# Layer 1's input convolution on four engines, and its sums of directions inside a list-scheduled output stage

## The chip, the cores and the metric

The kernel runs on one core of one Trainium2 chip. The metric is the device time of one execution in microseconds (us). Before the change three runs took 27333.85, 27416.35 and 27510.57 us, a median of 27416.35 us. One more execution was recorded by the hardware profiler, and every duration below is from that one.

The engines are TensorE (PE, and PEld for its weight loads), VectorE (DVE), ScalarE (ACT), GpSimd (POOL) and SyncE (SP). In this kernel SP issues the DMAs.

## The reference, cut to what matters

Two layers work on an image x of 4 x 128 x 128 pixels with 192 channels. Layer 0 is not touched by the change. Layer 1 is, in all of it but the scan over time:

```python
x = x + layer1(_gn(x))            # _gn: group norm over 32 groups of channels, per batch
# layer1(v):
xz = v @ in_proj_w;  x_ssm, z = xz[..., :C], xz[..., C:]       # C = 192
xc = silu(conv3x3_depthwise(x_ssm) + conv_b)                   # zero padding
# four directions: rows forward, rows backward, columns forward, columns backward
ys = scan(...)                                                 # 16 states a channel
y  = y0 + y1 + y2 + y3            # y2, y3 are scanned by columns, so they are transposed
y  = (y - mean_c(y)) / sqrt(var_c(y) + 1e-5) * ln_g + ln_b     # over the 192 channels
return (y * silu(z)) @ out_w
```

All arithmetic is float32.

## The kernel before, in words

The kernel is a row of stages. `transpose_in` turns the input to channels by pixels. `layer0` does layer 0. Then layer 1 begins: `in_conv` makes the convolved input `xc`, `scans` runs the four directions, `merge` adds the column directions to the row directions, and `layer1_out` does the norm, the gate and the output product. Data goes from stage to stage through DRAM.

Layer 1 has 192 channels, and a tile has 128 partitions. So two batches form a pair (`PAIRS` is 2), and their 2 x 192 channels make three blocks of 128 partitions: block 0 is channels 0 to 127 of the first batch, block 1 is channels 128 to 191 of the first batch in partitions 0 to 63 and those of the second in partitions 64 to 127, and block 2 is channels 0 to 127 of the second batch. A product over channels thus needs several terms for a block, `PAIR_TERMS`: two terms for blocks 0 and 2, three for block 1. The weights of a term are padded with zeros to 128 x 128 (`pair_pack`).

An image of 16384 pixels is cut into 16 chunks (`NCH`) of 8 rows, 1024 pixels (`T`).

`in_conv` loops over 2 pairs, 3 blocks and 16 chunks, so 96 chunks. For each it loads the source blocks with one row above and below, normalises them on VectorE (line 790), makes the product on TensorE (line 805, and line 816 for the two edge rows), copies it into a padded tile `xi` on ScalarE (lines 809 and 820), takes the nine taps of the convolution on VectorE (lines 823 and 829), takes the silu (line 833) and writes the result twice: straight away, and turned into a whole image `img` in memory (line 835), from which the columns are stored (line 839). GpSimd only zeroes the edges of `xi` (line 796).

`merge` loads a whole image of a column direction, and for each chunk loads the row direction, adds the two (line 1228) and stores the sum back. `layer1_out` loops over 2 pairs and 16 chunks, so 32 chunks with all three blocks each. A chunk has a mean over channels (line 210 through `mm`), a subtraction (1264), a square (1265), a mean of the squares (210), Ln and Exp for the inverse root (1270, 1271), a multiplication (1272), scale and shift (1275), the gate z (210, 1282, 1283), and the output product, which also adds x itself through an identity matrix (lines 1291 to 1301).

Work in `in_conv`, `merge` and `layer1_out` is ordered by the program text and by the pools' buffers. `layer0` and `scans` are ordered in another way: each lists its operations with an engine, an assumed cost and the tiles that it reads and writes, and class `Order` plays a list schedule with these costs; `emit` then writes the instructions of each engine in the order found. Each engine runs its own list strictly in order, SP's too: an instruction that waits holds up all behind it.

Of the kernel before, what the change touches and what calls it, by code (L numbers as in the profile page):

```python
# [10 lines left out]
F32 = mybir.dt.float32  # L11
AF = mybir.ActivationFunctionType
# [36 lines left out]
def flat(t):  # L49
    return t.rearrange("p a b -> p (a b)")  # L50


def rows(t):
    return t.rearrange("p (r w) -> p r w", w=W)
# [146 lines left out]
class Maker:  # L201
    def __init__(self, tc):
        self.tc, self.nc = tc, tc.nc

    def mm(self, out, terms):

        nc = self.nc
        for h in range(2):
            for i, (lhsT, rhs) in enumerate(terms):
                nc.tensor.matmul(  # L210
                    out[:, h], lhsT, rhs[:, h * 512 : (h + 1) * 512],
                    start=(i == 0), stop=(i == len(terms) - 1),
                )

    def softplus(self, pool, x, bias):

        l = pool.tile([128, T], F32, tag="sp_l", name="sp_l", bufs=2)
        self.nc.scalar.activation(l, x, AF.Softplus, bias=bias)
        return l
# [544 lines left out]
    def load_gn(self, pool, gn, p):  # L764
        t = pool.tile([128, 3, 2], F32, tag="gn", name="gn")
        for i in range(3):
            self.load_block(t[:, i], gn, p, i, slice(0, 2))
        return t

    def in_conv(self, x1T, gn, xc, win, vec):  # L770

        nc, tc = self.nc, self.tc
        with tc.tile_pool(name="p_1", bufs=1) as p1, tc.tile_pool(
            name="p_2", bufs=2
        ) as p2, tc.tile_pool(name="p_ps", bufs=2, space=PSUM) as ps:
            for p in range(PAIRS):
                gnt = self.load_gn(p2, gn, p)
                for i in range(3):
                    vt = vec[:, i % 2]
                    img = p1.tile([128, W, H], F32, tag="img", name="img")  # L780
                    for j in range(NCH):
                        r0 = R * j
                        lo, hi = max(r0 - 1, 0), min(r0 + R, H - 1)
                        wl, nr = lo - (r0 - 1), hi - lo + 1
                        terms = []
                        for t, src in PAIR_TERMS[i]:
                            xt = p2.tile([128, R + 2, W], F32, tag=f"x{src}", name=f"x{src}")
                            xv = xt[:, wl : wl + nr].rearrange("c r w -> c (r w)")
                            self.load_block(xv, x1T, p, src, slice(lo * W, (hi + 1) * W))
                            nc.vector.tensor_scalar(  # L790
                                xv, xv, gnt[:, src, 0:1], gnt[:, src, 1:2],
                                ALU.subtract, ALU.mult,
                            )
                            terms.append((win[:, t], xt))
                        xi = p2.tile([128, R + 2, W + 2], F32, tag="xi", name="xi")
                        nc.gpsimd.memset(xi[:, :, 0:1], 0.0)  # L796
                        nc.gpsimd.memset(xi[:, :, W + 1 : W + 2], 0.0)
                        if j == 0:
                            nc.gpsimd.memset(xi[:, 0, :], 0.0)
                        if j == NCH - 1:  # L800
                            nc.gpsimd.memset(xi[:, R + 1, :], 0.0)
                        g = ps.tile([128, 2, 512], F32, tag="g", name="g_xi")
                        for h in range(2):
                            for q, (lhsT, xt) in enumerate(terms):
                                nc.tensor.matmul(  # L805
                                    g[:, h], lhsT, xt[:, 1 + 4 * h : 5 + 4 * h],
                                    start=(q == 0), stop=(q == len(terms) - 1),
                                )
                        nc.scalar.copy(
                            xi[:, 1 : R + 1, 1 : W + 1],  # L810
                            g.rearrange("p h (r w) -> p (h r) w", w=W),
                        )
                        g = ps.tile([128, 2, 512], F32, tag="g", name="g_halo")
                        for n, wr in enumerate(wr for wr in (0, R + 1) if wl <= wr < wl + nr):
                            for q, (lhsT, xt) in enumerate(terms):
                                nc.tensor.matmul(
                                    g[:, n, :W], lhsT, xt[:, wr],
                                    start=(q == 0), stop=(q == len(terms) - 1),
                                )
                            nc.scalar.copy(xi[:, wr, 1 : W + 1], g[:, n, :W])  # L820
                        acc = p2.tile([128, T], F32, tag="acc", name="acc")
                        a3 = rows(acc)
                        nc.vector.tensor_scalar(
                            a3, xi[:, 1 : R + 1, 1 : W + 1],
                            vt[:, V1_CW + 4 : V1_CW + 5], None, ALU.mult,
                        )
                        for t in range(9):
                            if t != 4:
                                nc.vector.scalar_tensor_tensor(  # L829
                                    a3, xi[:, t // 3 : t // 3 + R, t % 3 : t % 3 + W],  # L830
                                    vt[:, V1_CW + t : V1_CW + t + 1], a3, ALU.mult, ALU.add,
                                )
                        nc.scalar.activation(acc, acc, AF.Silu, bias=vt[:, V1_CB : V1_CB + 1])
                        nc.sync.dma_start(xc[0][p][i][:, j * T : (j + 1) * T], acc)
                        nc.scalar.copy(
                            img[:, :, r0 : r0 + R], acc.rearrange("p (r w) -> p w r", w=W)
                        )
                    for j in range(NCH):
                        nc.sync.dma_start(
                            xc[1][p][i][:, j * T : (j + 1) * T],  # L840
                            img[:, R * j : R * (j + 1)].rearrange("p w h -> p (w h)"),
                        )
# [367 lines left out]
    def merge(self, y):  # L1210

        nc, tc = self.nc, self.tc
        with tc.tile_pool(name="m_2", bufs=2) as p2, tc.tile_pool(name="m_3", bufs=3) as p3:
            for p in range(PAIRS):
                for i in range(3):
                    img = p2.tile([128, W, H], F32, tag="img", name="img")
                    for c in range(4):
                        w = slice(c * W // 4, (c + 1) * W // 4)
                        nc.sync.dma_start(
                            img[:, w].rearrange("p w h -> p (w h)"),  # L1220
                            y[1][p][i][:, w.start * H : w.stop * H],
                        )
                    for j in range(NCH):
                        cols = slice(j * T, (j + 1) * T)
                        t = p3.tile([128, T], F32, tag="y", name="y")
                        nc.sync.dma_start(t, y[0][p][i][:, cols])
                        t3 = rows(t)
                        nc.vector.tensor_tensor(
                            t3, t3,
                            img[:, :, R * j : R * (j + 1)].rearrange("p w r -> p r w"), ALU.add,  # L1230
                        )
                        nc.sync.dma_start(y[0][p][i][:, cols], t)

    def layer1_out(self, y, x1T, gn, out, wz, avg, wout, vec, ident, eps):
        nc, tc = self.nc, self.tc
        with tc.tile_pool(name="s_2", bufs=2) as p2, tc.tile_pool(
            name="s_ps", bufs=2, space=PSUM
        ) as ps:
            for p in range(PAIRS):
                gnt = self.load_gn(p2, gn, p)  # L1240
                for j in range(NCH):
                    cols = slice(j * T, (j + 1) * T)
                    ys, x1, xn, sqs = [], [], [], []
                    for i in range(3):
                        yt = p2.tile([128, T], F32, tag=f"y{i}", name=f"y{i}")
                        nc.sync.dma_start(yt, y[p][i][:, cols])
                        ys.append(yt)
                        xt = p2.tile([128, T], F32, tag=f"x{i}", name=f"x{i}")
                        self.load_block(xt, x1T, p, i, cols)
                        x1.append(xt)  # L1250
# [248 lines left out]
```

## Time and profile before

| what | value |
|---|---|
| median of three runs | 27416.35 us |
| the profiled execution | 27483.88 us, its span 27482.1 us |
| `in_conv`, first normalisation to last image store | 6138 to 7453 us: 1315 us |
| `scans` | 7453 to 25190 us: 17737 us |
| `merge` | 25190 to 25680 us: 490 us |
| `layer1_out` | 25680 to 27482 us: 1802 us |
| PE busy over the span | 24406.1 us, 89% |
| DVE busy | 22279.5 us, 81% |
| ACT busy | 21227.8 us, 77% |
| POOL busy | 19417.1 us, 71% |

The bounds of the stages are read off the first and last instructions of their lines. The page gives for each group of instructions its line, engine, operation, tiles and shapes, the count, the busy time and the mean of one; matmuls of float32 leave two records each, so a count of 28 records is 14 matmuls. In a list of stretches, each row has the length, then the busy time of each engine with the number of instructions, then the granted TensorE clock as a share of full speed, the share of the DMA engines' time that was used and the rate in GB/s.

### The profile page before, as it was taken

The numbers are of one execution on the slowest core, as the hardware profiler recorded it, in microseconds if no ns is written. First come the engines' busy times: TensorE is split into PE (matmuls) and PEld (weight loads), VectorE is DVE, ScalarE is ACT, GpSimd is POOL, SyncE is SP. The second block draws the span as 40 slices with busy tenths as digits, with TensorE's granted clock in tenths as the row PEclk, the third lists the DMA queues.
The fourth block names the chain that finished last, engine by engine and source line by source line (L and its number), as shares of the span: only waits on it lengthen the run. The fifth ranks groups of instructions, "written<-read, shape, count | busy, mean of one in ns | idle before, by whom it ended". The sixth has DMA issues, their size and how long they took to land.

```text
span 27482.1 us, 440640 instructions
## 1 busy us (share of the span) xinstructions
PE 24406.1 (89%) x169976; PEld 9399.1 (34%) x169976; DVE 22279.5 (81%) x16004; ACT 21227.8 (77%) x24544; POOL 19417.1 (71%) x9258
## 2 busy tenths in 40 slices
PE   5999999994599999999999999999999999996699
PEld 3333333332233333333333333333333333332355
DVE  4888888889888899899888898889998898896222
ACT  5989898963378888788888888888888888884355
POOL 3777777730088888888888898888888888885000
PEclk7999999997789999899999999999999999997899
DMA  7999999995544445444444454444454444455422
GB/s 214 240 237 244 236 244 234 244 219 187 174 122 128 132 133 137 126 127 125 117 126 130 131 138 129 131 131 133 133 138 118 119 121 125 132 135 178 175 83 81
DMA packets 1672336, 4265.04 MB, mean 155 GB/s; under 512 B 239584, under 2 KB 388512, under 8 KB 1667168
## 3 DMA queue, kind: packets, MB, share of 16 engines
q1 hardware_dynamic: 1670240, 4236.84, 57.6%
q8 instruction: 1346, 22.05, 0.4%
q14 instruction: 750, 6.14, 0.1%
HBM read 3296.80 MB, written 939.10 MB: 154 GB/s over the span
## 4 chain that ended last, share of the span: by engine, by line
PE 37%; DVE 19%; ACT 13%; issue 6%; DMA 4%; POOL 2%; SPq 1%; DVEq 0%; POOLq 0%; ACTq 0%
DVE h L1108 13%; PE f L1075 13%; PE Y L1122 10%; ACT h L1086 6%; ACT dA L1102 3%; PE s L929 3%; PE s L952 2%; POOL hc L1114 2%; DVE acc L829 2%; PE hf L590 1%; DMA y<-y 1%; DVE D L1001 1%; PE g_mean L210 1%; DMA C<-cs 1%; PE s L995 1%
## 5 line engine op out<-in xcount | busy, mean ns | idle before, releaser
L1114 POOL TENSOR_TENSOR hc<-h,C 128x1024 f32<-128x1024 f32 x6144 | 14338.8, 2363 | 2382.5 <-PE Y L1122 1149.2
L1108 DVE TENSOR_TENSOR_SCAN h<-dA,st,h 128x1024 f32<-128x1024 f32 x5760 | 13132.8, 2333 | 765.5 <-ACT st L1138 281.2
L1086 ACT COPY h<-f 128x1024 f32<-128x1024 f32 (+3 forms) x8192 | 6334.2, 799 | 2215.8 <-PE f L1075 2144.5
L1075 PE MATMUL f<-D,dT 32*64 32x256 f32 x98304 | 7157.2, 408 | 786.1 <-ACT h L1086 640.4
L1122 PE MATMUL Y<-hc,sel 128*64 128x512 f32 x24576 | 6986.2, 656 | 470.4 <-POOL hc L1114 215.2
L1102 ACT ACTIVATE dA<-d,alog 128x1024 f32<-128x1024 f32 x6144 | 6905.3, 1124 | 312.3 <-DVE h L1108 257.1
L1075 PEld LDWEIGHTS f<-D,dT 32*64 32x64 f32 x98304 | 3276.9, 138 | 6683.6 <-ACT h L1086 4810.8
L468 POOL TENSOR_TENSOR xs<-xs,pr 128x1024 f32<-128x1024 f32 x1536 | 3637.3, 2371 | 341.0 <-ACT pr L463 251.4
L611 DVE SCALAR_TENSOR_TENSOR hf<-hh,vec,hf 128x512 f32<-128x512 f32 x3072 | 2318.3, 755 | 427.3 <-PE hf L590 268.1
L1122 PEld LDWEIGHTS Y<-hc,sel 128*64 128x64 f32 x24576 | 1321.0, 141 | 2966.3 <-issue 1795.9
L590 PE MATMUL hf<-sa,diag 96*32 96x512 f32 x18432 | 2157.4, 601 | 22.6 <-DMA sa<-hpad 20.2
L463 ACT ACTIVATE pr<-xi,vec 128x1024 f32<-128x1024 f32 x1536 | 1714.1, 1143 | 297.2 <-POOL xs L468 291.8
L1001 DVE TENSOR_TENSOR D<-s,mask 128x1024 f32<-128x1024 f32 x1024 | 1240.2, 1211 | 849.7 <-PE s L995 849.7
L590 PEld LDWEIGHTS hf<-sa,diag 96*32 96x32 f32 x18432 | 563.2, 109 | 1490.8 <-issue 1402.1
L796 POOL MEMSET xi<- 128x10 f32 x96 | 24.5, 255 | 1480.5 <-DVE acc L829 1224.5
L805 PE MATMUL g_xi<-x,wx 128*128 128x512 f32 x896 | 545.0, 745 | 590.5 <-DVE x L790 515.6
L550 POOL TENSOR_TENSOR dl<-dl,xs 128x1024 f32<-128x1024 f32 x192 | 454.6, 2368 | 832.8 <-ACT dA L548 745.8
L962 POOL TENSOR_TENSOR u<-l,u 128x1024 f32<-128x1024 f32 x384 | 907.4, 2363 | 184.6 <-ACT l L955 161.7
L829 DVE SCALAR_TENSOR_TENSOR acc<-xi,vec,acc 128x1024 f32<-128x1024 f32 x768 | 959.3, 1280 | 23.2 <-ACT xi L820 9.7
L1108 DVE TENSOR_TENSOR_SCAN h<-dA,h 128x1024 f32<-128x1024 f32 x384 | 856.2, 2274 | 59.5 <-ACT dA L1102 27.6
L952 PE MATMUL s<-pj,w 128*128 128x512 f32 x1536 | 894.2, 665 | 6.9 <-ACT l L955 2.2
L210 PE MATMUL g_mean<-y,avg 128*128 128x512 f32 x896 | 393.5, 596 | 480.3 <-DMA y<-y 480.0
(172 smaller groups left out, 23437.1 us busy)
## 6 DMA issues: line engine op xcount, KB each, us to landing
C<-cs SPq DMA_DIRECT2D x4096, 256.0 KB, 4.8
sa<-hpad SPq DMA_DIRECT2D x2304, 276.0 KB, 7.3
d<-delta SPq DMA_DIRECT2D x1536, 256.0 KB, 4.2
u<-xc SPq DMA_DIRECT2D x384, 512.0 KB, 4.7
delta<-l SPq DMA_DIRECT2D x384, 512.0 KB, 3.8
y<-y SPq DMA_DIRECT2D x1536, 128.0 KB, 3.3
hh<-hpad SPq DMA_DIRECT2D x384, 414.0 KB, 7.8
y<-y SPq DMA_DIRECT2D x288, 512.0 KB, 3.8
```

The source lines that it names most:

```text
L463: op("ACT", 1.1, lambda pr=pr, t=t: nc.scalar.activation(rows(pr()), x()[:, t // 3 : t // 3 + R, t % 3 : t % 3 + W], AF.Copy, scale=v(k, V ...
L468: op("POOL", 2.38, lambda pr=pr: nc.gpsimd.tensor_tensor(o(), o(), pr(), ALU.add), reads=[pr], writes=[o], early=-429)
L590: nc.tensor.matmul(o()[32 * g : 32 * g + 32], diag[:, d, s, k, g], x[:, g, :, c0 : c0 + W], start=(d == 0 and s == 0), stop=(d == 1 and s ...
L611: nc.vector.scalar_tensor_tensor(o3, hh()[:, 1 + dy : 5 + dy, PAD + dx : PAD + dx + W], v(k, V0_K + col), o3, ALU.mult, ALU.add,)
L829: nc.vector.scalar_tensor_tensor(a3, xi[:, t // 3 : t // 3 + R, t % 3 : t % 3 + W], vt[:, V1_CW + t : V1_CW + t + 1], a3, ALU.mult, ALU.add,)
L1001: nc.vector.tensor_tensor(t().rearrange("t a (n s) -> t (a n) s", s=32), g()[:, : 2 * NS].unsqueeze(2).to_broadcast([128, 2 * NS, 32]), ma ...
L1075: nc.tensor.matmul(gs()[64 * jn : 64 * jn + 64, n, 256 * a : 256 * a + 256], td()[rt, r // 64, 2 * sb + a], tD()[rt, a, 256 * jn : 256 * j ...
L1086: nc.scalar.copy(H[:, at : at + nq, 256 * sb : 256 * sb + 256].rearrange("p q (a r s) -> p q a r s", a=2, s=32)[:, :, :, 2 * rp : 2 * rp + 2],
L1102: op("ACT", 1.16, lambda: nc.scalar.activation(a(), d(), AF.Exp, scale=alog[:, c : c + 1]), reads=[d], writes=[a], table="exp", early=-522)
L1108: nc.vector.tensor_tensor_scan(hs[:, way], a()[:, way], hs[:, way], 0.0 if at == 0 else s0()[:, q : q + 1], ALU.mult, ALU.add,)
L1114: op("POOL", 2.4, lambda: nc.gpsimd.tensor_tensor(t(), hs, tC(), ALU.mult), reads=[hq, tC], writes=[t])
L1122: nc.tensor.matmul(ym()[64 * th : 64 * th + 64], sel, t()[:, 512 * th : 512 * th + 512], start=(q == 0), stop=(q == NQ - 1),)
```

## The change

Three stages are replaced by two: `in_conv` is written anew, and `merge` and `layer1_out` become one stage, `outputs`. Both are now ordered by `Order`. `layer0` and `scans` keep their text, and the order of every engine in them is the same as before.

In both stages the group norm is no longer applied to x. `pair_weights` multiplies the weights by the inverse deviation once for each pair, and forms the product of weights and mean, which becomes a bias at the eviction.

In `in_conv` a chunk now loads only eight new rows; the two rows that it shares with its predecessor are copied (`cy`). The nine taps are split: taps 0 and 8 on TensorE with diagonal weights into PSUM, taps 4, 1, 3, 5 and 7 on VectorE, the first of them adding the PSUM result, and taps 2 and 6 as products on ScalarE, which GpSimd adds up and then adds to the sum. The image `img` has two buffers in place of one. The tile `x` has one ring of four buffers for all source blocks.

In `outputs` the mean and the mean of squares are formed for each of the two batches, as 128 equal rows, in place of each of the three blocks: a whole-array matmul for the block of 128 channels, and for block 1 a matmul with the 64 rows of that batch. The two batches' 64-row matmuls follow each other. The gate's projection and the output product use 64-row matmuls for block 1 too, and the projection of block 1 uses two matmuls with 64 columns each. The mean is subtracted straight from PSUM, scale joins the multiplication by the inverse deviation, shift joins the gate. Ln and Exp are grouped for the two batches. `merge` for the first pair comes first, and that for the second pair is placed among the chunks of the first; the image has one buffer.

```diff
+    def pair_project(self, outs, i, terms, xs):
...
+        if i == 1:
+            parts = [(1, slice(0, 128), slice(0, 128)), (0, slice(0, 128), slice(0, 64)),
+                     (2, slice(0, 128), slice(64, 128))]
+        else:
+            parts = [(i, slice(0, 128), slice(0, 128)), (1, slice(32 * i, 32 * i + 64), slice(0, 128))]
+        of = {src: lhsT for lhsT, src in terms[i]}
+        for h, out in enumerate(outs):
+            for q, (src, k, m) in enumerate(parts):
+                nc.tensor.matmul(
+                    out[m], of[src][k, m], xs(src, h)[k], start=(q == 0), stop=(q > 0 if i == 1 else q == 1)
+                )
...
+    def in_conv(self, x1T, gn, xc, win, vec, ident):
...
+        TENSOR, PRODUCTS, VECTOR = (0, 8), (2, 6), (4, 1, 3, 5, 7)
...
+            od = Order(keep=226, idle=0.250, rate=300e3)
...
+                    t = xs[src] = buf("x", 4, 128, R + 1, W)
...
+                op("PE", 3.0, mm, reads=list(xs.values()), writes=[g, t], early=-150)
+                op("POOL", 0.5, edges, writes=[t])
...
+                op("PE", 3.2, taps_mm, reads=[t], writes=[gc])
+                op("DVE", 1.5, lambda: tap(VECTOR[0], flat(gc())), reads=[t, gc], writes=[acc])
+                for q in VECTOR[1:]:
+                    op("DVE", 1.3, lambda q=q: tap(q, acc()), reads=[t], writes=[acc])
+                prs = []
+                for q in PRODUCTS:
+                    pr = buf("pr", 3, 128, T)
+                    op("ACT", 1.12, lambda q=q, pr=pr: nc.scalar.activation(
+                        rows(pr()), shifted(q), AF.Copy, scale=vt[:, V1_CW + q : V1_CW + q + 1]),
+                        reads=[t], writes=[pr], early=30)
+                    prs.append(pr)
+                op("POOL", 2.4, lambda: nc.gpsimd.tensor_tensor(
+                    prs[0](), prs[0](), prs[1](), ALU.add), reads=[prs[1]], writes=[prs[0]])
+                op("POOL", 2.41, lambda: nc.gpsimd.tensor_tensor(
+                    acc(), acc(), prs[0](), ALU.add), reads=[prs[0]], writes=[acc])
+                op("ACT", 1.17, lambda: nc.scalar.activation(
+                    acc(), acc(), AF.Silu, bias=vt[:, V1_CB : V1_CB + 1]), writes=[acc])
+                op("SP", 0.1, lambda: nc.sync.dma_start(
+                    xc[0][p][i][:, j * T : (j + 1) * T], acc()), reads=[acc], size=524e3)
+                op("ACT", 2.02, lambda: nc.scalar.copy(
+                    img()[:, :, R * j : R * j + R], acc().rearrange("p (r w) -> p w r", w=W)
+                ), reads=[acc, img], writes=[(img, j)], early=-237)
...
-    def merge(self, y):
...
-    def layer1_out(self, y, x1T, gn, out, wz, avg, wout, vec, ident, eps):
...
+    def outputs(self, y, x1T, gn, out, win, wo, vec, ident, eps):
...
+            def merge(p, i):
+                img = buf("img", 1, 128, W, H)
...
+                    t = buf("m", 3, 128, T)
...
+                def averages(name, src):
+                    gs = [bank2(name), bank2(name)]
+
+                    def mm():
+                        for h in range(2):
+                            c = slice(512 * h, 512 * h + 512)
+                            for e in range(2):
+                                nc.tensor.matmul(
+                                    gs[e]()[:, h], avg, src[2 * e]()[:, c], start=True, stop=False
+                                )
+                            for e in range(2):
+                                k = slice(64 * e, 64 * e + 64)
+                                nc.tensor.matmul(
+                                    gs[e]()[:, h], avg[k], src[1]()[k, c], start=False, stop=True
+                                )
...
+                                nc.tensor.matmul(
+                                    dst[e], ys[2 * e]()[:, tok], wo[:, 0], start=True, stop=False
+                                )
+                                nc.tensor.matmul(
+                                    dst[e][:, 0:128], x1[2 * e]()[:, tok], ident,
+                                    start=False, stop=False,
+                                )
...
+                                nc.tensor.matmul(
+                                    dst[e], ys[1]()[k, tok], wo[k, 1 + e], start=False, stop=False
+                                )
...
+                                nc.tensor.matmul(
+                                    dst[e][:, 128:C], x1[1]()[k, tok], ident[k, k],
+                                    start=False, stop=True,
+                                )
...
+            for i in range(3):
+                merge(0, i)
+            for p in range(PAIRS):
+                for j in range(NCH):
+                    if p == 0 and j in (1, 6, 11):
+                        merge(1, j // 5)
+                    chunk(p, j)
```

## Prediction

> **What bounds the kernel now.** I first cut the span into stages by the lines of `in_conv`, `scans`, `merge` and `layer1_out`. The stretches give each engine's load.
>
> ```profile
> 6138.00:7453.00 1315.00, 649.27 (x1736) 318.68 (x1736) 1196.35 (x1088) 431.23 (x469) 30.46 (x199) 0.74 0.59 185
> 7453.00:25190.00 17737.00, 16256.19 (x133104) 5996.88 (x133104) 15701.72 (x8193) 14699.00 (x17595) 15210.40 (x6525) 0.94 0.48 128
> 25190.00:25680.00 490.00, 7.63 (x19) 1.46 (x18) 182.44 (x100) 1.12 (x1) 7.84 (x4) 0.50 0.83 313
> 25680.00:27482.00 1802.00, 1746.84 (x6784) 1061.68 (x6783) 424.33 (x384) 993.73 (x928) 0.00 (x0) 1.00 0.28 84
> ```
>
> (Columns: stretch, length, busy PE, PEld, DVE, ACT, POOL, clock, DMA share, GB/s.) Three stages have three bounds: VectorE in `in_conv` (1196 of 1315 us), DMA in `merge` (0.83, compute idle), TensorE in `layer1_out` (1747 of 1802). The change leaves the other 23,875 us as they are, with the same order of instructions, so all is decided in 3607 us: 1315 + 490 + 1802. The groups of the first stage say what VectorE does there:
>
> ```profile
> L829 DVE SCALAR_TENSOR_TENSOR acc<-xi,vec,acc 128x1024 f32<-128x1024 f32 x768 | 959.3, 1280 | 23.2 <-ACT xi L820 9.7 <-DVE acc L829 0.5
> ...
> L835 ACT COPY img<-acc 128x1024 f32<-128x1024 f32 x96 | 191.8, 2004 | 20.5 <-DMA xc<-acc 9.5 <-DMA xc<-img 9.2
> ...
> L790 DVE TENSOR_SCALAR x<-x,gn 128x1280 f32<-128x1280 f32 x196 | 184.3, 941 | 29.1 <-DMA x<-x1T 25.6 <-PE g_halo L816 3.5
> ```
>
> Eight taps a chunk, and 23 us of idle time before all 768: nothing is late. For what a small matmul costs, I read TensorE's timeline in `layer0`, which already runs 32-row matmuls:
>
> ```profile
> 3005.46 1.12 PE L499 MATMUL g<-proj,ident 32*128 32x512 f32 x2
> 3006.51 2.84 PE L649 MATMUL g<-y,avg 128*128 128x512 f32 x6
> ...
> 3017.32 1.13 PE L499 MATMUL f<-proj,ident 32*128 32x512 f32 x4
> 3018.38 2.84 PE L649 MATMUL g<-sq,avg 128*128 128x512 f32 x6
> ```
>
> One such matmul (2 records) takes 1.05 us to the next start, two on different rows (4 records) 1.06: pairs on different rows run together. The mean of `layer1_out`, 14 matmuls in 12.1 us, gives 0.86 us for a whole one. So a change of array shape costs about 0.2 us.
>
> Last, does GpSimd suffer beside VectorE? The edge zeroing of `in_conv` tells:
>
> ```profile
> 6708.38 7.25 DVE L829 SCALAR_TENSOR_TENSOR acc<-xi,vec,acc 128x1024 f32<-128x1024 f32 x6
> 6714.58 0.12 POOL L796 MEMSET xi<- 128x10 f32 x1 [13.76 <-DVE acc L829]
> ...
> 6650.49 0.75 DVE L823 TENSOR_SCALAR acc<-xi,vec 128x1024 f32<-128x1024 f32 x1
> ...
> 6650.72 0.57 POOL L796 MEMSET xi<- 128x10 f32 x1 [9.25 <-DVE acc L829]
> ```
>
> It takes 0.12 us beside a tap with two inputs in memory, and 0.57 beside a multiplication by a constant, until that ends.
>
> **What the Trainium skill says.** "TensorEngine Tiling (Array Packing)", Key Properties: tiles execute in parallel, and changing the mode drains the array. The lines above agree: 1.06 against 1.05, and 0.2 us. "TensorE: Matmul & The Clock Gate", Part 1: TensorE left idle falls to half clock. The stages agree: 0.74 where PE is half idle, 1.00 where full. "ScalarE: Activation LUTs", What ACT_TABLE_LOAD costs: 1283 ns and a drain of 1380; the trace has 1283 ns, and the chain shows no drain behind it. "GPSIMD Engine Reference", Key points: GpSimd contends with VectorE when that is in a two-port mode or has two SBUF inputs. The zeroing above bears out the first if L823 runs in such a mode, and not the second; but it only writes. No GpSimd *read* runs beside a two-input tap in the trace of before.
>
> **The change part by part: the convolution.** Per chunk, of 96:
> - VectorE loses three taps, L823 and 2.33 normalisations. Five taps stay; starts are 1.20 us apart (six in 7.25), so 6.0. The first reads PSUM: L611 does 512 elements so in 0.755 us, so at most 0.3 more; I take 6.1.
> - TensorE: projection four slots of 0.86 and four shape changes, 4.2; diagonal taps 4 x 0.86 = 3.4; together 7.7 at full clock. The gaps shrink, so I take full clock.
> - ScalarE: eviction 1.10 (L423), two row copies of 0.39 (L449, L453), two products of 1.14 (L463), silu 1.15, image 2.00: 7.3. The products and copies are new; all engines but TensorE hide them.
> - GpSimd: two sums of 2.37 (L468) and edges 0.2: 4.9.
> - DMA: before, 243.6 MB at 0.59 of 1315 us is 3.2 us a MB. Now 1.05 MB in, 1.05 out: 6.7.
>
> Four resources within 6.1 to 7.7 can't all be full. `scans`, scheduled likewise, has PE at 16,256 of 17,737 us, 92%. At 90% a chunk takes 8.5, 816 in all. To this I add waits. Block 1 needs three source tiles of a ring of four, three of which come free only at the projection's end; the refill of 1.05 MB (similar loads land in 6.3 us) and the next 4.2 make 10.5 or more, 2.5 x 32 = 80. Sixteen image stores stand ahead of loads on SP six times: 8.4 MB at 350 GB/s is 24 us, with about 12 covered by loaded tiles: 70. Weights at the start and the last stores: 45. Sum 1010, so **-305**. For GpSimd beside two-input taps the lower bound is 0; the upper is exclusion: 4 x 1.2 + 4.9 = 9.7 plus the first tap 1.3, 11 a chunk, 1075 plus 75 of waits, 140 more. I take 0 and keep 140.
>
> **The output stage.** TensorE per chunk, of 32: two averages, each twice (2 x 0.86, a pair 0.86, two changes 0.4), 11.9 where 24.2 stood. Gate 12.7 (six halves of 2 x 0.86 + 0.4), before 12.1. Output product: before, four matmuls with 576 columns take 1.10 us. Now per row of pixels 640 columns whole 1.22, pairs 256 columns 0.49, changes 0.4: 2.1 x 8 = 16.9, before 17.5. Sum 41.5 against 53.8. The gain is nearly all in the averages; shape changes eat the rest. The 64-row pairs do not show in the trace of before; the 32-row ones above stand for them (bounds: 0.86, and 1.72 if serial).
>
> ScalarE: three Square 1.06, two Ln 1.11, two Exp 1.06, three silu 1.02, four evictions 0.80, three table loads 1.28: 17.6, before 31. VectorE: eight batch operations and three gates at 1.22 (64 rows cost as 128), 13.4, and sums of directions 3 x 1.89: 19. DMA: 497 us in `layer1_out` (0.276 of 1802) and 407 in `merge`, 28 a chunk. All lie beside 41.5 of TensorE.
>
> Not all hides. VectorE's list has 36 direction sums ahead of the first subtraction: two whole images and four strips. An image took 79 us before (six in 472) with two buffers. With one, the next 8.4 MB (27 us at 313 GB/s) waits for the last sum; I take 88. Then 2 x 88 + 27 + 18 = 220 us with TensorE idle. Two chunks are then interleaved. TensorE waits about 5 us a pair for PSUM (a ring of three, taken two at a time) and loads, so 44 a chunk: 16 x 44 = 704 for the second pair. For the first, SP's stores and reloads of `m` (three buffers, a round of 4.3 us each way) stand ahead of the next y loads, and sums that wait hold VectorE's gates: I estimate 4 more, 768. Start, filling and end 40. Sum 1732 where 2292 stood: **-560**. If the sums hide wholly and waits vanish, 32 x 42 + 150 is 1494.
>
> **Sum.** -305 - 560 = -865: 27,484 - 865 = 26,619 for the profiled execution, which lies 68 us (0.25%) above the median. Against the median: **26,550 us**.
>
> **The rivals.**
> - *GpSimd excluded by two-input taps.* For: the skill, and that in every other stage VectorE's operations beside GpSimd take one input from PSUM. Against: the edge zeroing is not held up. +140: 26,690.
> - *64-row pairs run one after the other.* Averages 15.4, gate 14.5, product 20.8: 50.7, +9.2 x 32 = 294, and 55 in the convolution: 26,900. Against: L499's pair.
> - *All overlaps.* Convolution 850 (8.2 a chunk, 65 of waits), outputs 1500: 3607 - 2350 = 1257 saved: 26,160. For: TensorE's 97% in `layer1_out`.
> - *SP holds the convolution in series: slower.* A store of `acc` waits for the chain projection 4.2, eviction 1.1, taps 3.4, VectorE 6.1, GpSimd 4.8, silu 1.2, about 21 us, and later loads (6.3) stand behind it. One chunk in flight gives 27 us x 96 = 2600, +1285, and with -560 that is 28,140. It decides once a chunk passes (1315 + 560) / 96 = 19.5 us, so below 1.4 chunks in flight. Against: in SP's built order, loads run about four chunks ahead of their store.
>
> **How the numbers follow.** My forecast 0.58, exclusion 0.16, serial pairs 0.10, full overlap 0.12, series 0.04. About 1% is what a measurement of this kernel can tell from no change; all but the last case lie beyond it: faster 0.95, same 0.01, slower 0.04. The range 26,150 to 26,900 reaches from full overlap to serial pairs and holds exclusion; outside lie the series case, parts of the two end cases and the tails of my own guess at waits.
>
> **What would show it.** In the profile after: convolution stretch near 1010 us with PE at 70 to 75% and clock above 0.9; L790 gone; GpSimd's sums at 2.37 if I am right, above 3 if excluded. Outputs: about 220 us of idle TensorE, then 44 to 48 us a chunk; two 64-row matmuls in about 0.9 to 1.1 us. Wrong if SP's waits for stores show up as TensorE waiting for x or y in most chunks, if shape changes cost far from 0.2 us, or if VectorE waits for `m` ahead of gates for more than 10 us a pair.

## The result and the profile after

The changed kernel takes 26,404.5 us (median of four runs, 26,270.5 to 26,512.3) where the kernel before takes 27,447.3 us beside it (median of four). The ratio is 0.962, with a 95% interval of 0.956 to 0.968: **faster by 3.8%**. The prediction said 26,550 us, in a range of 26,150 to 26,900.

The profiled execution of the changed kernel has a span of 26,510.5 us. Three of its stretches answer to those shown of before (stretch, length, busy PE, PEld, DVE, ACT, POOL with instructions, clock, DMA share, GB/s). They are `in_conv`, `scans` and `outputs`:

```profile
6120.00:7140.00 1020.00, 825.85 (x1720) 283.91 (x1720) 837.48 (x500) 660.49 (x667) 520.57 (x396) 0.88 0.57 197
7140.00:24900.00 17760.00, 16283.17 (x133102) 6002.23 (x133104) 15700.14 (x8193) 14692.97 (x17595) 15205.52 (x6525) 0.94 0.47 128
24940.00:26510.00 1570.00, 1313.07 (x6004) 700.58 (x6002) 613.42 (x448) 556.36 (x543) 0.00 (x0) 0.93 0.57 188
```

The convolution has no engine near 100% any more: TensorE has 81%, VectorE 82%. In `scans` every sum agrees with before to 0.2%. The output stage is still bound by TensorE, but not in its first part, in which the sums of directions run alone:

```profile
24940.00:25130.00 190.00, 10.16 (x19) 2.72 (x18) 65.69 (x35) 1.11 (x1) 0.00 (x0) 0.53 0.87 319
25300.00:25770.00 470.00, 446.53 (x2002) 234.14 (x2001) 231.34 (x166) 192.34 (x188) 0.00 (x0) 0.99 0.73 246
25800.00:26470.00 670.00, 639.25 (x2908) 337.89 (x2907) 212.13 (x173) 275.61 (x269) 0.00 (x0) 0.99 0.38 113
```

To compare runs I cut each profiled execution at the same four events: the start of layer 0's last statistics, the start of the first VectorE operation of `scans`, the start of the last sum of y in `scans`, and the end of the span.

| run | layer 0 | convolution | scans | outputs | span |
|---|---|---|---|---|---|
| before | 6122.6 | 1334.9 | 17742.1 | 2282.5 | 27482.1 |
| after | 6112.4 | 1031.8 | 17766.9 | 1599.4 | 26510.5 |
| difference | -10 | **-303** | +25 | **-683** | -972 |

The runs below leave `layer0` and `scans` alone. In them an untouched convolution or output stage repeats within 15 us and layer 0 within 32, but `scans` varies between 17,568 and 17,767 us. So an edit of 50 us is read from its stage and not from the median of the whole.

In the convolution the groups of VectorE and GpSimd are the new thing. The last row has the shortest, median and longest of the same taps, in ns:

```profile
L896 DVE SCALAR_TENSOR_TENSOR acc<-xi,vec,acc 128x1024 f32<-128x1024 f32 x384 | 715.8, 1864 | 26.8
L912 POOL TENSOR_TENSOR pr<-pr 128x1024 f32<-128x1024 f32 x96 | 287.7, 2997 | 41.2 <-ACT pr L908 41.2
L914 POOL TENSOR_TENSOR acc<-acc,pr 128x1024 f32<-128x1024 f32 x96 | 225.7, 2351 | 435.9 <-issue 388.4 <-DVE acc L896 47.4
L896 DVE SCALAR_TENSOR_TENSOR acc<-xi,vec,c 128x1024 f32<-128x1024 f32 x96 | 122.5, 1276 | 126.2 <-PE c L890 123.5 <-DMA x<-x1T 2.7
...
L896 DVE SCALAR_TENSOR_TENSOR acc<-xi,vec,acc x384: 1283/1285/3476, 6154.8 to 7114.9; 128x1024 f32<-128x1024 f32 x192
```

The same tap took 1280 ns before and takes 1864 on average now, though the first of each chunk, which reads PSUM (`c`), takes 1276. The average hides two kinds: 228 of the 384 taps take 1.28 us as before, and a GpSimd sum runs during 0.02 us of them on average; the other 156 take up to 3.5 us, and a sum runs during 2.05 us of them on average. One GpSimd sum takes 2997 ns where 2370 is usual. The timeline of one chunk shows why (start, length, engine, line, operation):

```profile
6603.55 1.27 DVE L896 SCALAR_TENSOR_TENSOR acc<-xi,vec,c 128x1024 f32<-128x1024 f32 x1
6603.76 2.35 POOL L914 TENSOR_TENSOR acc<-acc,pr 128x1024 f32<-128x1024 f32 x1 [3.92 <-issue]
...
6604.86 8.35 DVE L896 SCALAR_TENSOR_TENSOR acc<-xi,vec,acc 128x1024 f32<-128x1024 f32 x4
...
6606.43 2.98 POOL L912 TENSOR_TENSOR pr<-pr 128x1024 f32<-128x1024 f32 x1
...
6613.12 1.27 DVE L896 SCALAR_TENSOR_TENSOR acc<-xi,vec,c 128x1024 f32<-128x1024 f32 x1
...
6613.34 2.35 POOL L914 TENSOR_TENSOR acc<-acc,pr 128x1024 f32<-128x1024 f32 x1 [3.93 <-issue]
```

Four taps with both inputs in memory take 8.35 us beside two sums, where six took 7.25 before. Taken one by one (the view joins them), they last 2.33, 3.20, 1.28 and 1.28 us: the first ends 1.08 us after the end of the first sum, the second 1.09 after the end of the other. The sum into `acc` needs the last tap of its chunk and starts 0.08 to 0.15 us after it in all 96 chunks, so it falls beside the next chunk's tap that reads PSUM, and isn't held up there. The two engines go in lock-step, 9.57 us from chunk to chunk.

### The profile page after: what moved, and what is told of

Its sections match the earlier page's. It is cut to its first block, busy times and chain, and to the rows that moved or that the text cites. A ratio compares the mean times of both kernels' runs of the same rounds, so it can differ in the third digit from the quotient of the medians.

```text
span 26510.5 us, 438073 instructions
## 1 busy us (share of the span) xinstructions
PE 24193.3 (91%) x169220; PEld 9017.9 (34%) x169220; DVE 21935.4 (83%) x15401; ACT 21016.8 (79%) x24359; POOL 19902.8 (75%) x9450
## 4 chain that ended last, share of the span: by engine, by line
PE 40%; DVE 18%; ACT 11%; issue 6%; DMA 4%; POOL 3%; SPq 0%; DVEq 0%; POOLq 0%; ACTq 0%
DVE h L1207 14%; PE f L1174 13%; PE Y L1221 11%; ACT h L1185 6%; PE s L1028 3%; ACT dA L1201 3%; POOL hc L1213 2%; PE s L1051 2%; DMA C<-cs 2%; PE z L785 1%; PE hf L574 1%; DVE D L1100 1%; DVE acc L896 1%; PE f L785 1%; PE s L1094 1%
## 5 line engine op out<-in xcount | busy, mean ns | idle before, releaser
L1028 PE MATMUL s<-u,w 128*128 128x512 f32 x1536 | 756.4, 630 | 53.3 <-DMA prev<-xc 52.6
L1054 ACT ACTIVATE l<-s,vec 128x512 f32<-128x512 f32 x768 | 527.8, 687 | 328.5 <-PE s L1051 323.9
L1094 PEld LDWEIGHTS s<-ident,pj 128*128 128x128 f32 x4096 | 554.1, 196 | 599.5 <-issue 256.7
L392 PE MATMUL f<-xa,w 96*128 96x512 f32 (+1 forms) x1536 | 724.8, 616 | 25.7 <-ACT xi L407 25.5
```

What stands on the lines that cost most here:

```text
L1028: nc.tensor.matmul(g(), wt()[:, 0, i], uu[i]()[:, 512 * c : 512 * c + 512], start=(i == 0), stop=(i == 2),)
```

## The experiments

**Theory.** VectorE's taps with two inputs in memory (SBUF) and GpSimd's sums take turns, and this sets the pace of the convolution; the output stage gains on TensorE, in part by its 64-row pairs, and pays for the sums of directions only at its start. **Rivals.** (a) The taps are slow for another reason (the chained read of `acc`, or TensorE and the loads set the pace anyway). (b) The pairs gain nothing. (c) The interleaved sums cost time in each chunk. (d) The list schedule is not needed.

### The two parts alone

`in_conv` and its weights from the changed kernel, the rest of before; and the other way round. The calls are shown:

```diff
-    mk.in_conv(x1T, gn1, xc, wx, vec)
+    mk.in_conv(x1T, gn1, xc, wx, vec, ident)
```

```diff
-    mk.merge(y)
-    mk.layer1_out(y[0], x1T, gn1, out, wz, avg, wout, vec, ident, eps)
+    mk.outputs(y, x1T, gn1, out, wz, wout, vec, ident, eps)
```

> Only the convolution is changed; sums of directions and output stage as before. From the marks in the two traces (last statistics of layer 0 to the first operation of the scans, 1335 to 1032 us): 303 us less than before, about 1.1%. If the parts act on each other (clock, DMA), it differs from that by over 80 us.

> Only the output stage with the sums is changed; the convolution as before. From the marks (last operation of the scans to the end, 2283 to 1599 us): 683 us less than before, about 2.5%. With the run of the convolution alone it should add up to the whole 972.

The convolution alone: 27,121.6 us, ratio 0.990 (0.986 to 0.993), its stage 1035.1, so -300. The outputs alone: 26,710.1 us, ratio 0.975 (0.971 to 0.979), their stage 1612.4, so -670. The medians lose 310 and 722 us, 1032 together, against 1043 for both parts at once. The parts add up, and `scans`, with 17,686 and 17,598 us, stays within its usual variation. Within a part no run separates the changes: what the norm in the weights, the split of the taps and the fewer loads each bring of the 300 us is not shown.

### Taps whose sum stays in PSUM

Four of the five taps add in place in the PSUM tile; only the last writes `acc`. No tap has two inputs in SBUF now. GpSimd's work is the same.

```diff
+                    out = acc() if q == VECTOR[-1] else flat(gc())
...
-                        rows(acc()), shifted(q), vt[:, V1_CW + q : V1_CW + q + 1], rows(into),
+                        rows(out), shifted(q), vt[:, V1_CW + q : V1_CW + q + 1], rows(into),
...
-                op("DVE", 1.5, lambda: tap(VECTOR[0], flat(gc())), reads=[t, gc], writes=[acc])
-                for q in VECTOR[1:]:
-                    op("DVE", 1.3, lambda q=q: tap(q, acc()), reads=[t], writes=[acc])
+                for q in VECTOR[:-1]:
+                    op("DVE", 1.5, lambda q=q: tap(q, flat(gc())), reads=[t], writes=[gc])
+                op("DVE", 1.3, lambda: tap(VECTOR[-1], flat(gc())), reads=[t, gc], writes=[acc])
```

> The new convolution, but VectorE's first four taps add up in PSUM (in place in the tile that TensorE's taps fill), and only the fifth writes to SBUF, so that no tap reads two SBUF tiles. Theory A, VectorE's two-input taps and GpSimd's sums exclude each other and their sum of 9.6 us bounds a chunk: the sums stay at 2.35 us and no tap is lengthened; VectorE needs 4 x 1.45 + 1.25 = 7.1 us a chunk, TensorE's 7.7 bounds, about 8.3 a chunk, the stage 96 x 8.3 + 95 = 890 us in place of 1032, the total about 140 us lower than the changed kernel. Theory B, waits for loads, stores and TensorE set about 10 us a chunk and long taps only fill them: the stage stays within 30 us of 1032.

The stage takes 946.3 us, 85 less (890 us was expected). The groups of this run, from 6200 to 7050 us:

```profile
L897 DVE SCALAR_TENSOR_TENSOR c<-xi,vec,c 128x1024 f32<-128x1024 f32 x371 | 478.0, 1288 | 253.1 <-PE c L890 212.9 <-ACT acc L917 13.0 <-ACT img L921 2.3
L913 POOL TENSOR_TENSOR pr<-pr 128x1024 f32<-128x1024 f32 x93 | 220.1, 2367 | 74.4 <-ACT pr L909 72.4 <-DMA x<-x1T 2.1
L915 POOL TENSOR_TENSOR acc<-acc,pr 128x1024 f32<-128x1024 f32 x92 | 216.9, 2358 | 332.1 <-issue 265.3 <-PE f L785 29.0 <-DVE acc L897 18.5
```

Taps are back at 1288 ns (1450 was expected) and both sums at 2360, running beside taps. VectorE now waits 213 us for TensorE's diagonal taps. In blocks 0 and 2 a steady chunk takes 7.65 us, all of it TensorE's: a projection of 4.11 and the two diagonal taps of 3.54 to the next start. The changed kernel has 9.58 there. In block 1 most chunks take 9.2 us in both kernels, of which TensorE stands idle for 1.58 between a chunk's projection and its diagonal taps.

From first tap to first tap, the two images of block 1 take 171 us each in the changed kernel and 172 and 173 here. All of the gain lies in the other four, 29, 17, 20 and 19 us. That is less than 64 x 1.93 = 124 us. A likely reason, which no run isolates, is that TensorE's waits for x near the changes of image (51 us, 43 in the changed kernel) now fall on the engine that sets the pace: the longest chunk of block 2 takes 26 us, where it took 19 and 21.

The median of the four executions, 26,378.7 us, has the ratio 0.962 of the changed kernel, so it does not show the 85 us; more executions follow below.

### GpSimd's sums left out

The control on the other side: the taps stay as they are, and GpSimd has nothing to add, so taps 2 and 6 don't reach the result.

```diff
-                op("POOL", 2.4, lambda: nc.gpsimd.tensor_tensor(
-                    prs[0](), prs[0](), prs[1](), ALU.add), reads=[prs[1]], writes=[prs[0]])
-                op("POOL", 2.41, lambda: nc.gpsimd.tensor_tensor(
-                    acc(), acc(), prs[0](), ALU.add), reads=[prs[0]], writes=[acc])
```

> Leaves out part of the computation: GpSimd's two sums, so taps 2 and 6 do not reach the result; ScalarE still makes the products. Theory A (exclusion): the taps fall back to 1.28 us, VectorE needs 6.1 us a chunk, TensorE's 7.7 us bound the stage, 96 x 8.2 + 95 = 880 us in place of 1032. Theory B (waits): within 30 us of 1032.

The stage takes 951.3 us, 81 less (880 was expected), and the two-input taps run at 1285 ns:

```profile
L896 DVE SCALAR_TENSOR_TENSOR acc<-xi,vec,acc 128x1024 f32<-128x1024 f32 x367 | 471.4, 1285 | 25.8
```

Slow taps need both: two inputs in SBUF and a busy GpSimd. Rival (a) falls, since the chained read of `acc` is still there. That this run and the last agree within 5 us says that turns, and not GpSimd's work, cost the 80 to 85 us.

### All seven taps on VectorE

```diff
-        TENSOR, PRODUCTS, VECTOR = (0, 8), (2, 6), (4, 1, 3, 5, 7)
+        TENSOR, VECTOR = (0, 8), (4, 1, 3, 5, 7, 2, 6)
...
```

The products on ScalarE and the two sums on GpSimd are gone.

> The new convolution without GpSimd's share: taps 2 and 6 are two more taps on VectorE, ScalarE's products and GpSimd's sums are gone. Theory A (exclusion): 1.27 + 6 x 1.2 = 8.5 us of VectorE a chunk, less than the 9.6 that taps and sums need in turn; the stage about 96 x 8.5 + 95 = 910 us, 120 less, although VectorE does more. Theory B (waits): VectorE's added 2.4 us make it slower or leave it at 1032.

A miss: 1063.9 us, 32 more than the changed kernel, where 910 was expected. (The medians, 26,371.9 and 26,404.5 us, don't tell the two apart.) The VectorE timeline of this run, where it is slow:

```profile
6608.75 8.02 DVE L896 SCALAR_TENSOR_TENSOR acc<-xi,vec,acc 128x1024 f32<-128x1024 f32 x6
6618.00 1.28 DVE L896 SCALAR_TENSOR_TENSOR acc<-xi,vec,c 128x1024 f32<-128x1024 f32 x1 [1.23 <-PE c L890]
6619.32 8.02 DVE L896 SCALAR_TENSOR_TENSOR acc<-xi,vec,acc 128x1024 f32<-128x1024 f32 x6
6628.98 1.28 DVE L896 SCALAR_TENSOR_TENSOR acc<-xi,vec,c 128x1024 f32<-128x1024 f32 x1 [1.63 <-PE c L890]
```

Six taps take 8.02 us, so 1.34 from start to start, where I had counted with 1.20. With the first tap that makes at least 9.3 us a chunk, and most chunks take just this. In blocks 0 and 2 others take 10.3 to 11.0, since the diagonal taps come up to 1.6 us late, as here. All six images take 2 to 14 us longer than in the changed kernel. Even with GpSimd hampered, handing it two taps is worth 32 us of the stage.

### The averages not paired

The two 64-row matmuls of a half no longer follow each other: each stands behind its whole-array one.

```diff
                                 nc.tensor.matmul(
                                     gs[e]()[:, h], avg, src[2 * e]()[:, c], start=True, stop=False
                                 )
-                            for e in range(2):
                                 k = slice(64 * e, 64 * e + 64)
```

> The averages of the output stage with the same matmuls in another order: each 64-row matmul directly follows the whole one of its batch, so that no two 64-row matmuls stand beside each other. If pairs run together and a change of array shape costs 0.2 us: a half goes from 2.97 to 4 x 0.86 + 4 x 0.2 = 4.24 us, four halves a chunk, 32 chunks: 163 us longer. If pairs gain nothing by standing together, only two more changes a half: 0.4 x 4 x 32 = 51 us longer. If changes of shape cost nothing in such a row, 0.86 x 4 x 32 = 110.

The output stage takes 1723.7 us, 124 more; the median is 26,543.0, ratio 0.968 (0.966 to 0.971). A half of the averages on TensorE's timeline, in the changed kernel:

```profile
26110.71 1.98 PE L1381 MATMUL f<-s,avg 128*128 128x512 f32 x4
26112.62 1.13 PE L1386 MATMUL f<-s,avg 64*128 64x512 f32 x4
26113.68 1.98 PE L1381 MATMUL f<-s,avg 128*128 128x512 f32 x4
```

and in this run:

```profile
26127.26 1.12 PE L1381 MATMUL f<-y,avg 128*128 128x512 f32 x2
26128.32 1.12 PE L1385 MATMUL f<-y,avg 64*128 64x512 f32 x2
26129.37 1.12 PE L1381 MATMUL f<-y,avg 128*128 128x512 f32 x2
26130.43 1.12 PE L1385 MATMUL f<-y,avg 64*128 64x512 f32 x2
26131.48 1.13 PE L1381 MATMUL f<-y,avg 128*128 128x512 f32 x2
```

Start to start, a half is 2.97 us paired and 4.22 unpaired: 1.25 more, which is one 64-row matmul (0.86) and two changes of shape (0.2 each). Four halves a chunk make 5.0, and 32 chunks 160 us, of which 124 reach the end. Rival (b) falls: a pair costs what one does. But the pairs are a small part of the gain: without them the stage is still 559 us shorter than before.

### The sums of directions left out

```diff
-            for i in range(3):
-                merge(0, i)
             for p in range(PAIRS):
                 for j in range(NCH):
-                    if p == 0 and j in (1, 6, 11):
-                        merge(1, j // 5)
                     chunk(p, j)
```

> Leaves out part of the computation: the sums of directions, so the output stage reads the row directions alone and moves 151 MB less. If the sums cost only the start, in which TensorE waits for the first two images (about 190 us): the stage falls from 1599 to about 1410 us. If, as I predicted, the sums among the first 16 chunks also hold them up by 4 us each: to about 1345.

The stage takes 1400.5 us, 199 less. In the changed kernel TensorE does three gate blocks and the first matmuls of its first mean early, and then waits for the sums of the other blocks. It goes on 219 us after the last operation of `scans`, and the wait is named on its row of the timeline:

```profile
25129.77 2.08 PE L1381 MATMUL f<-y,avg 128*128 128x512 f32 x2 [160.74 <-DMA y<-y]
```

Without the sums the first mean starts 15 us after that operation, 204 sooner. The output stores show that two chunks take 85 to 87 us with the sums (once 90) and without them. The cost is nearly all at the start, and rival (c) falls.

### The convolution in the order of the text

The same operations, issued as the program lists them, not in the order that `Order` finds.

```diff
...
-                self.span2 = od.emit()
+                self.span2 = od.emit(listed=False)
```

> The new convolution with each engine's instructions in the order in which the program lists them, not in the list schedule's: on SP the store of a chunk stands ahead of the next chunk's loads. The slow rival of the prediction: one chunk in flight, about 27 us a chunk, 96 of them 2600 us, so some 1560 us more than the changed kernel, near 27,960. It would be wrong if a chunk takes under 19.5 us, where the order of SP would not decide the sign.

The stage takes 3093.2 us, and the one run 28,538.8 us: **slower than before by 4%**. TensorE's timeline of this run, in block 1:

```profile
6800.19 7.08 PE L791 MATMUL f<-x,x0w 128*128 128x512 f32 x12 [18.26 <-DMA x<-x1T]
6808.86 3.67 PE L896 MATMUL c<-xi,diag 128*128 128x512 f32 x8 [1.58 <-issue]
6830.67 5.61 PE L791 MATMUL f<-x,x0w 128*128 128x512 f32 x12 [18.14 <-DMA x<-x1T]
6837.85 3.67 PE L896 MATMUL c<-xi,diag 128*128 128x512 f32 x8 [1.58 <-issue]
6859.29 6.60 PE L791 MATMUL f<-x,x0w 128*128 128x512 f32 x12 [17.77 <-DMA x<-x1T]
```

```profile
6823.00 0.33 SPq L924 DMA_DIRECT2D xc<-acc  x1
6823.42 2.50 SPq L833 DMA_DIRECT2D x<-x1T  x4
```

TensorE waits 18 us for x in every chunk: the load stands behind the store of the chunk before in SP's queue (the second view). In the first pair a chunk takes 29 to 31 us, and 32 on average with the changes of image in. The projection, 4.1 us in the runs above, takes 5.6 to 7.1 here; the granted clock over the stage is 0.62. The slow rival of the prediction is real, at more than the 27 us that I gave it, and rival (d) falls for the convolution: the order is worth 2060 us there. The output stage was not tried in the order of the text.

### The better version, more closely, and a fifth source tile

The changed kernel and the PSUM taps again with six executions each on one chip, with a third kernel that has both the PSUM taps and a ring of five source tiles; one product buffer had to go to make room.

```diff
-                    t = xs[src] = buf("x", 4, 128, R + 1, W)
+                    t = xs[src] = buf("x", 5, 128, R + 1, W)
...
-                    pr = buf("pr", 3, 128, T)
+                    pr = buf("pr", 2, 128, T)
```

> The changed kernel itself, in more rounds, beside the next two on the same chip. The first measurement gave a ratio of 0.9622 with 0.6% on either side; with more executions I expect 0.962 to 0.965 and half the interval.

> The kernel with the four VectorE taps in place in PSUM again, in more rounds. If the 85 us that its convolution stage gained reach the end, its ratio lies 0.003 below that of the changed kernel (27,440 us times 0.003 is 85). If the convolution's gain is given back in the scans, the two agree to 0.001.

> The same, with a ring of five source tiles instead of four (one buffer fewer for products makes the room). In the run with four, TensorE waits four times for x in the convolution, 18, 7, 19 and 7 us, 52 in all, and SP issues 16 image stores in 18 us ahead of the load that ends the first of these waits. If the ring of three-source blocks causes the waits, one tile more takes a good part of them away: a stage of about 910 us instead of 946. If the burst of image stores in SP's queue causes them, one tile more covers at most one more load: 935 to 950.

| kernel | median | ratio to before (27,431.4) | convolution |
|---|---|---|---|
| changed kernel | 26,445.3 | 0.9643 (0.9616 to 0.9670) | 1030.9 |
| PSUM taps | 26,342.5 | 0.9612 (0.9588 to 0.9637) | 944.7 |
| PSUM taps, ring of five | 26,344.1 | 0.9609 (0.9580 to 0.9638) | 959.7 |

The ratio falls by 0.0031, as forecast. From the six executions of each, the means differ by 84 us, with a 95% interval of about 62 on either side. That agrees with the stage's 86 us reaching the end, though the first four executions of each differ by 26 us only, in the median. The PSUM taps beat both kernels: 3.9% faster than before.

On balance the fifth tile does not help: 960 us, 15 more, and 10 above what even the burst of stores let me expect. What TensorE waits for with four tiles is shown by SP's queue and TensorE's timeline of the PSUM-taps run at a change of image:

```profile
6314.52 15.35 SPq L931 DMA_DIRECT2D xc<-img  x16
6330.81 0.32 SPq L919 DMA_DIRECT2D xc<-acc  x1
6332.08 4.52 SPq L827 DMA_DIRECT2D x<-x1T  x4
```

```profile
6343.57 6.29 PE L785 MATMUL f<-x,x0w 128*128 128x512 f32 x12 [18.16 <-DMA x<-x1T]
6511.57 16.07 PE L785 MATMUL f<-x,x0w 128*128 128x512 f32 x16 [7.12 <-DMA x<-x1T]
...
6788.42 5.77 PE L785 MATMUL f<-x,x1w 128*128 128x512 f32 x12 [17.91 <-DMA x<-x1T]
6955.39 16.07 PE L785 MATMUL f<-x,x1w 128*128 128x512 f32 x16 [6.69 <-DMA x<-x1T]
```

The four long waits, 50 us in all, stand at changes of image, behind 16 image stores that hold SP for 15 to 18.5 us; elsewhere in block 1 TensorE waits for x hardly at all. With five tiles these waits are 13, 3, 13 and 3 us, and the sum of all waits for x falls only from 50 to 39.

Block by block the fifth tile does two things. The two images of block 1 go from 172 and 171 us to 156 and 154: TensorE's idle time before the diagonal taps falls from 22 us to 5 in each. But the other images lose 50 us, with 9.1 to 9.4 us a chunk. There TensorE's list now often has three projections in a row, and the diagonal taps wait 35 us in all for VectorE to free their PSUM tile, which they don't do with four tiles. Whether that comes from the product buffer that was taken away was not tried.

## Why the prediction was right, and where its steps were off

The size came out: both stages gained, 303 us where 305 was forecast and 683 where 560 was. In the output stage that is for the reasons given; in the convolution it is in part luck. The median of 26,404.5 us lies 146 below the forecast, and 123 of these are the output stage's. The steps beneath are less good than the sum.

**Convolution, -305 against -303: two errors that cancel.** That they cancel to 2 us is luck. The sum was 8.5 us for each of 96 chunks, 816, and 195 of waits. In the trace a chunk takes 9.58 us in 64 cases and about 9.7 in 32 (without the long wait of each image), 924 together, which leaves 108 of 1032 for everything else.
- "I take 0 and keep 140" failed. GpSimd is excluded by two-input taps: 81 us by leaving out its sums, 85 by moving the taps to PSUM. The bound of 140 was too high. Its sum has a slip: 96 x 11 is 1056 and not 1075, which makes 120. And it put all of GpSimd's work end to end with the taps, while one sum starts under each chunk's PSUM tap, and block 1 loses nothing to the turns. The evidence that I weighed against it was a zeroing of edges, which only writes; I said so and took 0 all the same. The Trainium skill, "GPSIMD Engine Reference", Key points, names this case, VectorE with two SBUF inputs, and it was right where I went against it: 1.28 us became 1.86 on average. The sign that I had named, GpSimd's sums above 3 us, hardly shows it: they average 3.00 and 2.35, and the taps were stretched instead.
- "80 (block-1 refill)" was too much. Outside the changes of image TensorE's waits for x in block 1 are below 2 us each in the changed kernel. What the ring of four costs there showed in the run with five, as 33 us in two images (with the PSUM taps). Of "70" for image stores, TensorE's waits for x at changes of image show 43 us.
- Without exclusion, the case I had forecast, the stage takes 946 and not 1010. The 8.5 us was near: 64 x 7.65 + 32 x 9.19 is 784. So in that run the waits were 162 instead of 195, and the chunk 0.3 us cheaper. My 90% was too low for blocks 0 and 2, where TensorE is full.
- "I take full clock": 0.88. After waits of about 7 us the projections ran at half speed (last section).

**Outputs, -560 against -683: right in mechanism, the terms 133 too large.**

| term | predicted | measured |
|---|---|---|
| start, TensorE idle | 220 | 219 |
| first pair, a chunk | 48 | 43 |
| second pair, a chunk | 44 | 42.7 |
| start, filling, end | 40 | about 9 (what is left) |

The start is right to 1 us, by two small errors: two images took 163 us where I had 176, and the time before the first sum and after the second image was 56 where I had 45. The term that was mis-sized most is the "4 more" of the first pair: the interleaved sums cost almost nothing beside TensorE (43.3 us a chunk with them, 43.0 without), so 5 us x 16 = 80 too many. The second pair gives 21, the end 31. TensorE's chunk is 40.4 us, not 41.5: a half of the averages takes 2.97 us (2.98 predicted), a block of the gate 4.2 (4.24), but a row of pixels in the output product 1.98 instead of 2.11. (The last 10 us are the stage before, 2282 by these marks where the prediction had 2292.) About 270 us of the gain come from the sums, which took 490 by themselves, and about 410 from shorter chunks.

**The rivals.** Exclusion: true as a mechanism, and hidden in the sum by my waits. Serial pairs: false, by 2.97 against 4.22. Full overlap: 850 and 1500 were forecast; the PSUM taps bring the convolution to 946, so part of that was there to be had, and the output stage has 1599. (With the sums left out it takes 1400, but that does less work.) SP in series: true for the order of the text, and only for that.

## What to carry to other kernels

Before you split elementwise work between VectorE and GpSimd, look where VectorE's inputs lie: here an accumulator in PSUM cost the same (1288 ns against 1285) and left GpSimd free, and one in SBUF made the two take turns. Price TensorE work from the timeline, start to start and with its changes of shape, for that step held to 3% here. Work laid under a full engine cost little more here than what had to precede that engine's first operation. The chain across five engines was worth nothing without an order in which the loads run ahead of the stores in the same queue: the same operations took 1032 us in one order and 3093 in the other.

## What was not expected of the hardware

- The turns between VectorE and GpSimd appear in this trace as longer instructions, not as idle time, and a mean hides them: 156 of 384 taps were stretched, to at most 3.5 us, and the others kept their 1.28. The 388 us of idle time with no releaser ("issue") before GpSimd's other sum are no sign of turns: that sum follows the last tap of its chunk within 0.15 us, and 267 us of the idle time stay when the taps add up in PSUM. A zeroing of 128x10 beside such taps keeps its 0.11 to 0.12 us.
- After waits of 6.7 to 7.6 us the next two projections ran at half speed: 16 records took 16.07 us, where 16 took 8.40 just before. With the ring of five, waits of 3.1 and 3.2 us were followed by 14.6 and 16.1 us. But after waits of 14 to 18 us the next 12 records, the projection of block 1, took 5.8 to 7.0 us instead of 4.1, so the length of the wait alone does not decide. The Trainium skill, "TensorE: Matmul & The Clock Gate", Part 1, says that an idle TensorE falls to half clock; the granted clock in the changed kernel was 0.50 over just these 16 us:

```profile
6470.00:6500.00 30.00, 30.00 (x64) 10.87 (x64) 23.43 (x16) 21.19 (x23) 16.30 (x14) 1.00 0.84 322
6500.00:6508.40 8.40, 1.65 (x4) 0.38 (x2) 8.16 (x5) 5.71 (x6) 5.64 (x2) 0.73 1.01 327
6508.40:6524.50 16.10, 16.07 (x17) 4.07 (x17) 11.44 (x7) 8.40 (x8) 9.94 (x8) 0.50 0.51 175
```

- `scans` differs by up to 200 us between executions of the same instructions, so the medians of single kernels need many runs before 80 us show.
